# A mixture-of-experts macaron layer: windows of rows from anywhere in the first expert stage, outputs stored in place and gathered by token

## The chip, the cores and the metric

One core of a Trainium2 chip runs the whole program. The metric is the device time of one execution, in microseconds (us), as the median of several runs.

## The reference

The layer is a macaron: half a feed-forward, attention, half a feed-forward, each with its residual. `x` has 8 blocks of 512 tokens with 128 features in float32.

```python
x = x + 0.5 * ffn(layernorm(x))
x = x + attn(layernorm(x))
x = x + 0.5 * ffn(layernorm(x))
```

`attn` works in windows of 128 tokens: q, k, v, scores, the 32 largest scores of each row kept, softmax, values, a leaky ReLU, residual and layer norm. `ffn` is a mixture of eight experts with a shared one: a layer norm, a router of 8 logits, the two best experts of each token with softmax gates,

```python
for e in range(E):
    y = _swiglu(normed, gate_up_w[e], down_w[e])
    out = out + comb[:, e, None] * y
out = out + _swiglu(normed, shared_gate_up_w, shared_down_w)
```

where a routed expert has 384 hidden features. `comb` is zero for all but two experts of a token, so the kernel computes each expert on its own tokens only.

## The kernel before

**Stages.** The tokens are cut into two groups `g` of 4 blocks (2048 tokens). An expert stage is named `(key, g)`: `key` 0 is the feed-forward before attention, 1 the one after it. The stages run in the order (0,0), (0,1), (1,0), (1,1). Attention of group 0 lies beside stage (0,1), attention of group 1 beside stage (1,0). The shared expert (`shared`, L573) and the norms (`norm`, L532) are placed among them as filling.

**Routing** (`route`, L593). For the 2048 tokens of a group there are 4096 (token, expert) entries. They are sorted by expert into 4096 slots, that is `NS` = 32 tiles of 128 slots. VectorE (DVE) works out each expert's count (`cnt`), its first and last slot (`from_`, `last`), the slot of each entry (`pos`), and for each slot the token (`src`, L742). A tile can hold slots of several experts, so the work is a list of `NT` = 39 pairs (tile, expert), which covers every case. For each pair, DVE works out the expert's offsets (`row`, `off`), the tile's first column (`to`, which is `r.at`), and for each of its 128 rows the place where the output goes (`dst`, L826, from the chain `second`, `sx`, `held`, `sel`, `what`, `away`, L797 to L826).

**An expert stage** (`experts`, L832, and `pair`, L875). Per tile, GpSimd (POOL) issues an indirect DMA that gathers 128 normed token rows of 512 B from DRAM into `xg` (L846, four buffers of four tiles each). TensorE (PE) transposes them (`xTp`, L858), ScalarE (ACT) applies gamma and beta and writes them into `xT` (L863), which holds all 32 tiles of the stage. Per pair, PE multiplies the expert's gate and up weights `wt` with 128 columns of `xT` from column `r.at` (L924, three matmuls of 128x128 for `pg` and three for `pu`), ACT takes the silu (`s`, L932), DVE multiplies by up (L935), and PE multiplies by the down weights `ew` (`y`, L940). Stages (0,0) and (1,1) get `wt` by a DVE copy from a copy of all weights in SBUF (L899); the other two by a DMA on SyncE's queue, SP (L901). After four pairs ACT copies `y` to `yb` (L954), the last seven pairs one by one. Then POOL issues one indirect DMA per pair, the put (L962), which scatters the 128 rows of `yb` to the places in `dst`: row `1 + k*2048 + token` for a token's first or second expert. Rows of a pair that belong to another expert go to spare rows. After a put without other POOL work, a one-element memset stands before the next (L960).

**Back to the tokens.** `fetch_back` (L972) reads the two output rows of each token of a block with two plain DMAs of 256 KB, on SP for stage (0,0). They wait for all 39 puts. `combine` (L990, L999) adds them to `x` with the gates as factors, on DVE. `attention` and `norm(1, b)` follow for the block.

**What sets the order.** Every operation is handed to a planner (`Plan`, L96) with an engine, a cost, the operations that it needs and a due time. A list scheduler (`schedule`, L144) runs them on modelled engines, and the order that comes out is the order of each engine's queue on the chip. The queue of each engine is in order: a waiting instruction holds all behind it. The costs are in the calls (an indirect DMA on POOL: 1.28 for a gather, 1.33 for a put), the due times in the constants of L62 to L69: `PACE` spaces the gathers of the four stages, `LAG` the blocks of the attention, `SHARED`, `SHARED1`, `NORM_*`, `ROUTE_*`, `PAIRS`, `PUTS` and `FINISH` place the rest. Where the plan sees PE idle for long, it puts in matmuls whose result nobody reads (`unread`, L448).

```python
before_[2] = pool(1.28, fetch, [r.src, *rows], [(xg, j)], lat=3.6,
                  after=[(before_[2], pace)])
plan.op("POOL", 1.33, put, [(yb, i), r.dst], [(group, c * CH + i)], lat=3.4)
```

Of the kernel before, what the change touches and what calls it, by code (L numbers as in the profile page):

```python
# [8 lines left out]
F32 = mybir.dt.float32  # L9
F16 = mybir.dt.float16  # L10
U32 = mybir.dt.uint32
# [8 lines left out]
W = 4  # L20
# [24 lines left out]
COPIED = ((0, 0), (1, 1))  # L45
LAST = 4
LAST_ON_PE = (4, 6)

# [3 lines left out]
OVERLAP = {"PE": 0.0, "ACT": 0.08, "DVE": 0.07, "POOL": 0.0, "SP": 0.0}  # L52
TABLE_LOAD = 1.28
COLD, COLD_FACTOR = 26.0, 1.8

# [5 lines left out]

PACE = (1.79, 2.74, 2.27, 0.89)  # L62
LAG, STRETCH, ROUTE_STRETCH = 9.73, -0.34, 3.22
NORM_B, NORM_LAG, NORM_STRETCH = 7.11, 1.83, 1.14
SHARED = ((28.42, 6.74), (33.75, 24.46))
SHARED1 = ((114.02, 8.44), (5.88, 23.46))
ROUTE_B = 38.08
PAIRS, PUTS = 0.5, 4.89
FINISH = 18.87  # L69

# [182 lines left out]
def kernel(  # L253
# [35 lines left out]
                for t in (  # L289
                    "mx", "sm", "m0", "m1", "i0", "pr", "eq", "o0", "o1", "th", "own", "cnt",  # L290
                    "upto", "last", "from", "at", "posf", "pos", "lo", "hi", "lo2", "hi2", "hot",
                    "signed", "second", "held", "sx", "tl", "pairs", "end", "whose", "ex", "back",
                    "tile", "sel", "what", "away",
                )
# [11 lines left out]
    def dve(us, fn, r, w, **k):  # L306
        return plan.op("DVE", us, fn, r, w, **k)
# [95 lines left out]

    xT = const.tile([P, NS * P], F32, tag="xT", name="xT")
    zero = const.tile([1, H], F32, tag="zero", name="zero")
# [116 lines left out]
    def begin(key, g):  # L522


        r = routed[key, g] = Routing()
        r.rows = dram.tile([1 + GT, H], F32, tag=f"n{key}{g}", name=f"rows_{key}_{g}")
        r.ys = dram.tile([1 + 2 * GT + NTP * P, H], F32, tag=f"y{key}{g}", name=f"ys_{key}_{g}")
# [65 lines left out]
    def route(key, g):  # L593
# [124 lines left out]
        for q in range(0, 2 * GW, part):  # L718
# [29 lines left out]
        end, back = t("end", [P, 1, NE]), t("back", [P, NTP, 1])  # L748
        dve(0.17, lambda: ve.tensor_scalar(
            tl()[:, 0, :], last()[:, 0, :], float(P - 1), None, ALU.add), [last], [(tl, 0)])  # L750
        dve(0.17, lambda: ve.tensor_copy(tl()[:, 1, :], from_()[:, 0, :]), [from_], [(tl, 1)])
        dve(0.17, lambda: ve.tensor_scalar(tl(), tl(), 7, None, ALU.logical_shift_right),
            [(tl, 0), (tl, 1)], [(tl, 0), (tl, 1)])
        dve(0.17, lambda: ve.tensor_tensor(
            pairs()[:, 0, :], tl()[:, 0, :], tl()[:, 1, :], ALU.subtract),
            [(tl, 0), (tl, 1)], [pairs])
        dve(0.17, lambda: ve.scalar_tensor_tensor(
            pairs()[:, 0, :], cnt()[:, :, 0], 0.0, pairs()[:, 0, :], ALU.is_gt, ALU.mult),
            [cnt, pairs], [pairs])
        dve(0.22, lambda: ve.tensor_tensor(  # L760
# [4 lines left out]
            [end, pairs], [pairs])  # L765
        dve(0.17, lambda: ve.tensor_tensor(
            pairs()[:, 0, :], pairs()[:, 0, :], tl()[:, 1, :], ALU.subtract),
            [pairs, (tl, 1)], [pairs])
        dve(0.17, lambda: ve.tensor_tensor(
# [18 lines left out]
        dve(0.49, lambda: ve.tensor_reduce(back()[:, :, 0], whose(), AX.X, ALU.add),  # L788
            [whose], [back])
        dve(0.18, lambda: ve.tensor_tensor(  # L790
            tile_(), tno[:, :, 0], back()[:, :, 0], ALU.subtract), [back], [tile_])
# [16 lines left out]

        sel, what, away = t("sel", wide), t("what", [P, NTP]), t("away", [P, NTP])
        dst = r.dst = t("dst", [P, NTP], U32)  # L810
# [21 lines left out]
    def experts(key, g, pace):  # L832
# [7 lines left out]
        for c, n in enumerate(sizes):  # L840
            t0 = sum(sizes[:c])
            xg = buf([P, CH, H], "xg", f"xg_{nm}_{c}")
            for j in range(n):

                def fetch(t=t0 + j, j=j, xg=xg):
                    nc.gpsimd.indirect_dma_start(  # L846
                        xg()[:, j, :], None, r.rows,
                        bass.IndirectOffsetOnAxis(ap=r.src()[:, t : t + 1], axis=0),
                    )

                before_[2] = pool(1.28, fetch, [r.src, *rows], [(xg, j)], lat=3.6,
                                  after=[(before_[2], pace)])
                fetched.append(before_[2])
# [21 lines left out]
    def pair(r, key, g, t, pace, came, first, upto):  # L875
# [33 lines left out]

        lo, hi = max(0, first - NE + 1), min(upto, NS) - 1  # L910

        def up(p, c):
            if c == 0 and t == first:
# [5 lines left out]
                    )[1]  # L919
                    for to, a, b in ((r.off, 0, (NE - 1) * FF), (r.at, lo * P, hi * P))  # L920
                ]
# [29 lines left out]
        else:  # L951
# [3 lines left out]
            [(y, i) for i in range(a, b)], [(yb, i) for i in range(a, b)],  # L955
        )
        for i in range(a, b):
            def put(t=c * CH + i, i=i):
# [10 lines left out]

            plan.op("POOL", 1.33, put, [(yb, i), r.dst], [(group, c * CH + i)], lat=3.4)  # L970

    def fetch_back(key, b):  # L972
# [5 lines left out]
            buf([P, W, H], f"a{k + 1}" if key else "yg", f"yg_{key}_{b}_{k}") for k in range(2)  # L978
        ]
        ys_t = r.ys[1 : 1 + 2 * GT, :].rearrange("(k b p w) h -> b k p w h", k=2, p=P, w=W)  # L980
        written = [(f"ys_{key}_{g}", t) for t in range(NT)]
        for k in range(2):
# [7 lines left out]
    def combine(key, b, yg):  # L990
# [4 lines left out]
        for k in range(2):  # L995
# [7 lines left out]

            dve(1.5, run, [yg[k], (gates, k), xk], [xk])

# [228 lines left out]
```

## Time and profile before

| | |
|---|---|
| median of 6 runs | 641.13 us (638.38 to 648.55) |
| the profiled execution: its own time | 646.61 us |
| its span, first to last instruction | 644.8 us |
| granted TensorE clock, mean | 0.947 |
| busy | PE 532.0, weight loads 484.8, DVE 376.7, ACT 274.7, POOL 366.6 us |
| indirect DMAs on POOL | 128 gathers (L846), 156 puts (L962) |

By the times of their instructions the stages lie about here: routing and start until 42 us; (0,0) from 42 to 193 us, the last put at 193.45; (0,1) with attention of group 0 until 332; (1,0) with attention of group 1 until 494; (1,1) until 626; then the last outputs. The timeline lists an instruction with its start, its duration, its engine and line, its tiles, and in brackets the idle time of its engine before it with what ended that. A PE matmul's end is modelled, not measured.

### The profile page before, as it was taken

How to read it: one execution, taken by the hardware profiler on the slowest of the kernel's cores; microseconds unless marked ns; L12 is line 12 of the kernel's file. 1: busy time of each engine (PE TensorE's matmuls, PEld its weight loads, DVE VectorE, ACT ScalarE, POOL GpSimd, SP SyncE). 2: the span in 40 equal slices, each digit the busy share in tenths (PEclk: the TensorE clock that was granted, in tenths of full speed). 3: DMA queues.
4: the chain of work that ended last, by engine and by line, in shares of the span. 5: the costliest groups of instructions: out<-in, count | busy, mean ns of one | idle time of the engine just before them, and what ended most of it. 6: DMA issues, size and time to landing. Idle time of an engine off the chain costs nothing.

```text
span 644.8 us, 13493 instructions
## 1 busy us (share of the span) xinstructions
PE 532.0 (82%) x4064; PEld 484.8 (75%) x4064; DVE 376.7 (58%) x1440; ACT 274.7 (43%) x588; POOL 366.6 (57%) x484
## 2 busy tenths in 40 slices
PE   4996977686894999899998999898988486679986
PEld 3885867585783978789878788797877386669976
DVE  6594623564330788896498999773585254324412
ACT  5712312121231469787521688875542021222320
POOL 6136536454564578768636878686256446555450
PEclk9898978788998999999999999999899798899999
DMA  7911111101134844437536453456542312111016
GB/s 216 336 54 50 30 30 38 30 28 34 34 114 131 260 131 125 134 109 209 176 127 194 127 160 104 149 161 195 148 144 81 127 58 79 34 34 34 26 38 196
DMA packets 39611, 72.27 MB, mean 112 GB/s; under 512 B 7604, under 2 KB 17848, under 8 KB 39544
## 3 DMA queue, kind: packets, MB, share of 16 engines
q1 hardware_dynamic: 29880, 51.73, 26.2%
q0 software_dynamic: 9088, 18.63, 9.3%
q10 hardware_dynamic: 576, 1.05, 0.5%
q8 instruction: 38, 0.62, 0.4%
q14 instruction: 29, 0.24, 0.1%
HBM read 54.86 MB, written 16.52 MB: 111 GB/s over the span
## 4 chain that ended last, share of the span: by engine, by line
PE 58%; DVE 15%; another core or an unknown queue 8%; issue 6%; ACT 6%; DMA 3%; POOL 3%; DVEq 0%; SPq 0%; POOLq 0%; ACTq 0%
PE y L940 15%; PE pg L924 14%; PE pu L924 13%; DVE s L935 3%; PE ysh L588 2%; PE pus L582 2%; PE xTp L858 2%; PE pgs L579 2%; PE lg L563 2%; DVE wt L899 2%; POOL ys L962 2%; DVE tk L1088 1%; DMA yg<-ys 1%; DVE x L999 1%
## 5 line engine op out<-in xcount | busy, mean ns | idle before, releaser
L962 POOL DMA_INDIRECT ys<-yb,dst x156 | 158.8, 1018 | 170.2 <-ACT yb L954 144.3
L940 PE MATMUL y<-ew,s 128*128 x936 | 142.8, 293 | 65.9 <-DVE s L935 54.2
L940 PEld LDWEIGHTS y<-ew,s 128*128 128x128 f32 x936 | 126.0, 204 | 78.2 <-DVE s L935 46.4
L846 POOL DMA_INDIRECT xg<-rows,src x128 | 127.1, 993 | 68.0 <-issue 34.8
L932 ACT ACTIVATE s<-pg 128x384 f32<-128x384 f32 x156 | 75.2, 490 | 191.2 <-PE pg L924 73.4
L924 PE MATMUL pg<-xT,wt 128*128 (+1 forms) x936 | 138.5, 286 | 14.9 <-ACT xT L863 7.8
L924 PEld LDWEIGHTS pg<-xT,wt 128*128 128x128 f32 x936 | 122.9, 199 | 23.5 <-issue 11.0
L924 PE MATMUL pu<-xT,wt 128*128 (+1 forms) x936 | 134.1, 281 | 0.9 <-DVE s L935 0.9
L899 DVE COPY wt<-egu 128x768 f32 x78 | 44.4, 570 | 139.8 <-PE pu L924 57.6
L924 PEld LDWEIGHTS pu<-xT,wt 128*128 128x128 f32 x936 | 121.1, 197 | 2.1 <-DVE s L935 1.1
L935 DVE TENSOR_TENSOR s<-pu,s 128x384 f32<-128x384 f32 x156 | 85.0, 550 | 58.3 <-PE pu L924 20.8
L954 ACT COPY yb<-y 128x512 f32<-128x512 f32 (+1 forms) x60 | 26.1, 436 | 54.2 <-PE y L940 31.8
L999 DVE SCALAR_TENSOR_TENSOR x<-yg,gates,x 128x128 f32<-128x128 f32 x112 | 35.5, 380 | 12.2 <-DMA yg<-ys 12.2
L863 ACT ACTIVATE xT<-xTp,gb 128x512 f32<-128x512 f32 (+2 forms) x34 | 25.4, 753 | 32.0 <-PE xTp L858 25.2
L448 PEld LDWEIGHTS unread<-ident 128*128 128x128 f32 x264 | 31.0, 192 | 1.9 <-issue 1.9
L448 PE MATMUL unread<-ident 128*128 128x128 f32 x264 | 31.8, 275 | 0.0
L1088 DVE MATCH_REPLACE8 tk<-am,tk 128x128 f32<-128x128 f32 x96 | 25.3, 273 | 0.0
L499 ACT ACTIVATE n<-x,nb,rstd 128x128 f32<-128x128 f32 x56 | 22.8, 485 | 4.5 <-DVE nb L479 4.5
L563 PEld LDWEIGHTS lg<-rwT,nT 128*128 128x128 f32 x128 | 19.7, 236 | 6.4 <-ACT nT L554 5.8
L858 PE MATMUL xTp<-ident,xg 128*128 128x128 f32 x128 | 22.2, 298 | 2.5 <-DMA xg<-rows,src 1.4
L563 PE MATMUL lg<-rwT,nT 128*128 128x8 f32 x128 | 19.7, 284 | 4.3 <-ACT nT L554 4.3
L581 ACT ACTIVATE ss<-pgs 128x512 f32<-128x512 f32 x16 | 9.5, 596 | 28.0 <-PE pgs L579 20.1
(177 smaller groups left out, 698.1 us busy)
## 6 DMA issues: line engine op xcount, KB each, us to landing
wt<-in_expert_gu SPq DMA_DIRECT2D x78, 384.0 KB
yg<-ys SPq DMA_DIRECT2D x28, 256.0 KB
rows<-n SPq DMA_DIRECT2D x16, 256.0 KB
egu<-in_expert_gu SPq DMA_DIRECT2D x8, 384.0 KB
ys<-yb,dst POOLq DMA_INDIRECT x156
x<-in_x SPq DMA_DIRECT2D x8, 256.0 KB
xg<-rows,src POOLq DMA_INDIRECT x128
out_x<-x SPq DMA_DIRECT2D x8, 256.0 KB
```

The costliest lines, as they stand in the source:

```text
L448: plan.idle = lambda: nc.tensor.matmul(unread, ident, ident, start=True, stop=True)
L563: nc.tensor.matmul(lg()[:, w, 0:NE], nT()[:, w, :], rwT, start=True, stop=True)
L846: nc.gpsimd.indirect_dma_start(xg()[:, j, :], None, r.rows, bass.IndirectOffsetOnAxis(ap=r.src()[:, t : t + 1], axis=0),)
L858: nc.tensor.transpose(tp()[:, w, :], xg()[:, w, :], ident)
L899: nc.vector.tensor_copy(to, egu[:, bass.ds(row, 2 * FF)])
L924: nc.tensor.matmul(p()[:, f, :], wt()[:, c * NF + f, :], xT[:, bass.ds(offs[1], P)], start=True, stop=True,)
L932: act(0.49, lambda: nc.scalar.activation(s(), pg()[:, 0:NF, :], AF.Silu), [pg], [s], table="silu")
L935: dve(0.56, lambda: nc.vector.tensor_tensor(s(), pu()[:, 0:NF, :], s(), ALU.mult), [pu, s], [s])
L940: nc.tensor.matmul(y()[:, j, :], s()[:, f, :], ew[:, bass.ds(offs[0] + f * H, H)], start=(f == 0), stop=(f == NF - 1),)
L962: ins = nc.gpsimd.indirect_dma_start(r.ys, bass.IndirectOffsetOnAxis(ap=r.dst()[:, t : t + 1], axis=0), yb()[:, i, :], None,).ins
L999: nc.vector.scalar_tensor_tensor(xs[b][:, w, :], yg[k]()[:, w, :], gates()[:, k, q : q + 1], xs[b][:, w, :], ALU.mult, ALU.add,)
L1088: ve.match_replace(tk()[:, w, :], m8()[:, w, :], src()[:, w, :], TAKEN)
```

## The change

In stage (0,0) alone (`WINDOWS`):

- A pair is no longer a tile with one of its experts. It is a window of 128 consecutive slots that begins anywhere: expert e gets `ceil(cnt/128)` windows, which begin at its first slot. There are still `NT` = 39 windows. `to` is then a column of `xT` that need not be a multiple of 128, and `xT` gets 128 more columns, zeroed.
- All 128 output rows of a window are stored where the window stands in the list: `ys` has 39 * 128 rows, and a plain DMA on SP writes a chunk of four windows at once (the last seven alone). The 39 puts of this stage go.
- `route` leaves out the chain of `dst` in this stage. Instead it adds to the slot of each entry what its expert's windows are shifted by, and keeps the two rows of each token in `want`.
- `fetch_back` gathers by `want`: for each block 2 x 4 indirect DMAs on POOL of 128 rows, 32 in all, in place of 8 plain DMAs. `combine` waits for the four gathers of its half.

The planner's cost of every indirect DMA, in all stages, becomes 1.72 (`INDIRECT`) for 1.28 and 1.33, and the due times are others. So the order of the instructions changes in all stages. `sel` shares its buffer with `whose`.

```diff
+WINDOWS = ((0, 0),)
+INDIRECT = 1.72
-PACE = (1.79, 2.74, 2.27, 0.89)
-LAG, STRETCH, ROUTE_STRETCH = 9.73, -0.34, 3.22
-NORM_B, NORM_LAG, NORM_STRETCH = 7.11, 1.83, 1.14
-SHARED = ((28.42, 6.74), (33.75, 24.46))
-SHARED1 = ((114.02, 8.44), (5.88, 23.46))
-ROUTE_B = 38.08
-PAIRS, PUTS = 0.5, 4.89
-FINISH = 18.87
+PACE = (1.79, 3.63, 1.5, 1.75)
+LAG, STRETCH, ROUTE_STRETCH = 10.08, -1.11, 7.26
+NORM_B, NORM_LAG, NORM_STRETCH = 11.74, 1.11, 2.32
+SHARED = ((28.42, 5.57), (35.54, 33.74))
+SHARED1 = ((73.75, 8.44), (5.88, 23.46))
+ROUTE_B = 34.16
+PAIRS, PUTS = -0.52, 2.74
+FINISH = 6.94
...
-    xT = const.tile([P, NS * P], F32, tag="xT", name="xT")
+    xT = const.tile([P, (NS + 1) * P], F32, tag="xT", name="xT")
+    nc.gpsimd.memset(xT[:, NS * P :], 0.0)
...
+        if r.windows:
+            dve(0.18, lambda: ve.scalar_tensor_tensor(
+                tile_(), tno[:, :, 0], float(P), back()[:, :, 0], ALU.mult, ALU.subtract),
+                [back], [tile_])
+            dve(0.18, lambda: ve.tensor_scalar(
+                to(), tile_(), float(NS * P), None, ALU.min), [tile_], [to])
+            plan.floor = max(floor, found.due + PUTS)
+            dve(B, lambda: ve.tensor_tensor(
+                at(), at(), pairs().to_broadcast(full), ALU.add), [at, pairs], [at])
+            for k, o in ((0, o0), (1, o1)):
+                dve(B, lambda o=o: ve.tensor_tensor(eq(), o(), at(), ALU.mult), [o, at], [eq])
+                dve(B, lambda k=k: ve.tensor_reduce(posf()[:, k, :], eq(), AX.X, ALU.add),
+                    [eq], [(posf, k)])
+            want = r.want = t("want", [P, 2 * GW, 1], U32)
+            before_[3] = dve(0.18, lambda: ve.tensor_copy(
+                want()[:, :, 0], posf().rearrange("p k w -> p (k w)")),
+                [(posf, 0), (posf, 1)], [want])
+            return
...
-                before_[2] = pool(1.28, fetch, [r.src, *rows], [(xg, j)], lat=3.6,
+                before_[2] = pool(INDIRECT, fetch, [r.src, *rows], [(xg, j)], lat=3.6,
...
+        if r.windows:
+            to = r.ys[(c * CH + a) * P : (c * CH + b) * P, :].rearrange("(i p) h -> p i h", p=P)
+            load(0.6, lambda: to, lambda: yb()[:, a:b, :], [(yb, i) for i in range(a, b)],
+                 [(group, c * CH + i) for i in range(a, b)], lat=3.0)
+            return
...
-            plan.op("POOL", 1.33, put, [(yb, i), r.dst], [(group, c * CH + i)], lat=3.4)
+            plan.op("POOL", INDIRECT, put, [(yb, i), r.dst], [(group, c * CH + i)], lat=3.4)
...
+        if r.windows:
+            for k in range(2):
+                for w in range(W):
+                    def fetch(k=k, w=w, q=k * GW + i * W + w):
+                        nc.gpsimd.indirect_dma_start(
+                            yg[k]()[:, w, :], None, r.ys,
+                            bass.IndirectOffsetOnAxis(ap=r.want()[:, q, :], axis=0),
+                        )
+                    pool(INDIRECT, fetch, [r.want, *written], [(yg[k], w)], lat=3.6)
+            return yg
...
-            dve(1.5, run, [yg[k], (gates, k), xk], [xk])
+            came = [(yg[k], w) for w in range(W)] if routed[key, g].windows else [yg[k]]
+            dve(1.5, run, [*came, (gates, k), xk], [xk])
```

More of the change, by code (lines that the diff above doesn't have):

```diff
@@ L292 @@
                     "signed", "second", "held", "sx", "tl", "pairs", "end", "whose", "ex", "back",
-                    "tile", "sel", "what", "away",
+                    "tile", "what", "away", "want",
                 )
@@ L526, in begin @@
         r.rows = dram.tile([1 + GT, H], F32, tag=f"n{key}{g}", name=f"rows_{key}_{g}")
-        r.ys = dram.tile([1 + 2 * GT + NTP * P, H], F32, tag=f"y{key}{g}", name=f"ys_{key}_{g}")
+        r.windows = (key, g) in WINDOWS
+        n = NT * P if r.windows else 1 + 2 * GT + NTP * P
+        r.ys = dram.tile([n, H], F32, tag=f"y{key}{g}", name=f"ys_{key}_{g}")
         load(0.3, lambda: r.rows[0:1, :], lambda: zero, (), [("rows", key, g, -1)], lat=3.0)
@@ L748, in route @@
         end, back = t("end", [P, 1, NE]), t("back", [P, NTP, 1])
[L749 to L759, printed above, removed]
+        if r.windows:
+            dve(0.17, lambda: ve.tensor_scalar(
+                tl()[:, 0, :], cnt()[:, :, 0], float(P - 1), None, ALU.add), [cnt], [(tl, 0)])
+            dve(0.17, lambda: ve.tensor_scalar(
+                tl()[:, 0, :], tl()[:, 0, :], 7, None, ALU.logical_shift_right),
+                [(tl, 0)], [(tl, 0)])
+            dve(0.17, lambda: ve.tensor_copy(pairs()[:, 0, :], tl()[:, 0, :]), [(tl, 0)], [pairs])
+        else:
+            dve(0.17, lambda: ve.tensor_scalar(
+                tl()[:, 0, :], last()[:, 0, :], float(P - 1), None, ALU.add), [last], [(tl, 0)])
+            dve(0.17, lambda: ve.tensor_copy(tl()[:, 1, :], from_()[:, 0, :]), [from_], [(tl, 1)])
+            dve(0.17, lambda: ve.tensor_scalar(tl(), tl(), 7, None, ALU.logical_shift_right),
+                [(tl, 0), (tl, 1)], [(tl, 0), (tl, 1)])
+            dve(0.17, lambda: ve.tensor_tensor(
+                pairs()[:, 0, :], tl()[:, 0, :], tl()[:, 1, :], ALU.subtract),
+                [(tl, 0), (tl, 1)], [pairs])
+            dve(0.17, lambda: ve.scalar_tensor_tensor(
+                pairs()[:, 0, :], cnt()[:, :, 0], 0.0, pairs()[:, 0, :], ALU.is_gt, ALU.mult),
+                [cnt, pairs], [pairs])
         dve(0.22, lambda: ve.tensor_tensor(
@@ L765, in route @@
             [end, pairs], [pairs])
-        dve(0.17, lambda: ve.tensor_tensor(
-            pairs()[:, 0, :], pairs()[:, 0, :], tl()[:, 1, :], ALU.subtract),
-            [pairs, (tl, 1)], [pairs])
+        if r.windows:
+            dve(0.17, lambda: ve.scalar_tensor_tensor(
+                pairs()[:, 0, :], pairs()[:, 0, :], float(P), from_()[:, 0, :],
+                ALU.mult, ALU.subtract), [pairs, from_], [pairs])
+        else:
+            dve(0.17, lambda: ve.tensor_tensor(
+                pairs()[:, 0, :], pairs()[:, 0, :], tl()[:, 1, :], ALU.subtract),
+                [pairs, (tl, 1)], [pairs])
         dve(0.17, lambda: ve.tensor_tensor(
@@ L789, in route @@
             [whose], [back])
+        if r.windows:
[15 more added lines that the diff above has]
+                [(posf, 0), (posf, 1)], [want])
+            plan.floor = floor
+            return
         dve(0.18, lambda: ve.tensor_tensor(
@@ L807, in route @@
             [signed, second], ["held"])
-        sel, what, away = t("sel", wide), t("what", [P, NTP]), t("away", [P, NTP])
+        sel, what, away = whose, t("what", [P, NTP]), t("away", [P, NTP])
         dst = r.dst = t("dst", [P, NTP], U32)
@@ L910, in pair @@
         lo, hi = max(0, first - NE + 1), min(upto, NS) - 1
+        end = P * min(NS, upto - 1) if r.windows else P * hi
         def up(p, c):
@@ L919, in up @@
                     )[1]
-                    for to, a, b in ((r.off, 0, (NE - 1) * FF), (r.at, lo * P, hi * P))
+                    for to, a, b in ((r.off, 0, (NE - 1) * FF), (r.at, lo * P, end))
                 ]
@@ L956, in pair @@
         )
+        if r.windows:
+            to = r.ys[(c * CH + a) * P : (c * CH + b) * P, :].rearrange("(i p) h -> p i h", p=P)
+            load(0.6, lambda: to, lambda: yb()[:, a:b, :], [(yb, i) for i in range(a, b)],
+                 [(group, c * CH + i) for i in range(a, b)], lat=3.0)
+            return
         for i in range(a, b):
@@ L979, in fetch_back @@
         ]
+        written = [(f"ys_{key}_{g}", t) for t in range(NT)]
+        if r.windows:
+            for k in range(2):
[7 more added lines that the diff above has]
+            return yg
         ys_t = r.ys[1 : 1 + 2 * GT, :].rearrange("(k b p w) h -> b k p w h", k=2, p=P, w=W)
-        written = [(f"ys_{key}_{g}", t) for t in range(NT)]
         for k in range(2):
```

## The prediction, made before the change was run

> **What bounds the kernel now.** I read the page first: engine shares, then the groups of the two indirect DMAs.
>
> ```profile
> PE 532.0 (82%) x4064; PEld 484.8 (75%) x4064; DVE 376.7 (58%) x1440; ACT 274.7 (43%) x588; POOL 366.6 (57%) x484
> PEclk9898978788998999999999999999899798899999
> L962 POOL DMA_INDIRECT ys<-yb,dst x156 | 158.8, 1018 | 170.2 <-ACT yb L954 144.3
> L846 POOL DMA_INDIRECT xg<-rows,src x128 | 127.1, 993 | 68.0 <-issue 34.8
> ```
>
> PE is the busiest, with a full clock in the middle and a lower one in the first and last expert stage. A put or a gather takes about 1.0 us and 0.3 us of issue, and puts mostly wait for ACT: POOL looks like no bound. Then the busy times by stage, for the stretches 42 to 193 us, stage (0,0), and 193 to 332 us, stage (0,1) with attention:
>
> ```profile
> 42.00:193.00 151.00, 117.80 (x865) 106.24 (x864) 68.82 (x179) 39.30 (x75) 82.84 (x107) 0.91 0.14 43
> 193.00:332.00 139.00, 123.84 (x962) 111.81 (x961) 98.81 (x439) 87.31 (x191) 92.81 (x113) 0.98 0.51 156
> ```
>
> In (0,0) no engine is full (PE 118 of 151 us, clock 0.91, although DVE has 69 and POOL 83). So I looked at what happens around one chunk, in the timeline of POOL, ACT and DVE:
>
> ```profile
> 148.25 1.08 POOL L962 DMA_INDIRECT ys<-yb,dst  x1 [0.22 <-issue]
> 149.63 1.01 POOL L846 DMA_INDIRECT xg<-rows,src  x1 [0.30 <-issue]
> 150.95 0.96 POOL L846 DMA_INDIRECT xg<-rows,src  x1 [0.31 <-issue]
> 152.21 0.94 POOL L846 DMA_INDIRECT xg<-rows,src  x1 [0.30 <-issue]
> 152.94 0.49 ACT L932 ACTIVATE s<-pg 128x384 f32<-128x384 f32 x1 [5.99 <-PE pu L924]
> 153.46 0.94 POOL L846 DMA_INDIRECT xg<-rows,src  x1 [0.30 <-issue]
> 155.83 0.56 DVE L899 COPY wt<-egu 128x768 f32 x1 [5.01 <-remote]
> 155.96 0.49 ACT L932 ACTIVATE s<-pg 128x384 f32<-128x384 f32 x1 [2.53 <-remote]
> ```
>
> While POOL issues eight indirect DMAs without a pause (144.4 to 154.4 us), ACT idles 6.0 and 2.5 us and DVE 5.0 us, although the matmuls that they wait for stand as done. The trace's record of semaphore updates says why: PE's semaphore doesn't rise from 148.6 to 152.9 and from 152.9 to 155.8 us, and then several times within 0.2 us. Set beside POOL's unbroken runs, such silences follow their length: runs of 7, 9, 7, 8 and 7 in this stage have 7.3, 5.8, 7.3, 7.2 and 7.3 us of silence, runs of 4 in (1,1) 0 to 3.0 us, in multiples of some 2.9 us. Why it is so the trace doesn't show; I use it as a relation. PE can go on for a while, then starves. From 42 to 206 us its pauses between matmul starts of over 1.5 us sum to 35.5 us. Seven stretches at clock 0.5 follow them, 34.1 us in all, worth half, 17.1. Together 52.6 us.
>
> The end of the stage, in SP's timeline and the chain:
>
> ```profile
> 184.53 21.08 SPq L901 DMA_DIRECT2D wt<-in_expert_gu  x5
> 205.72 0.84 SPq L317 DMA_DIRECT2D yg<-ys  x2
> ```
>
> ```profile
> 197.35 7.91 another core or an unknown queue
> ```
>
> The last put is issued at 193.45, but the read-back stands behind weight loads in SP's queue until 205.72, and the first combine runs at 212.27.
>
> **The change part by part.**
>
> (a) *39 puts go from POOL in (0,0).* From 42 to 206 us POOL issues 87 indirect DMAs: 39 puts and 48 gathers, 16 of them for (0,1). Puts and gathers join into runs of 7 to 9; without puts a chunk has a run of about 4. By share, 39/87 of 52.6 is 23.6 us. Lower end, nothing: puts were hidden and the silences stay with the gathers. Upper end, by runs of 4 in (1,1) (PE pauses of 1.65, 1.56 and 1.61 us, clock 1.0): about 45.8 us over 8 chunks is 5.7 each, 1.6 would remain, 33 gained. I take 24, the share in the stage itself.
>
> (b) *Handover.* Before, the last `yb` copy ends at 191.95 and the first combine starts at 212.27: 20.3 us. After: one store on SP (0.4 issue, landing as in the read issued at 213.43 and landed at 215.9, 2.5), eight gathers at 1.26 (to the start of the last, 8.8) and 2.4 to landing (gather at 115.12, complete by 117.5): 14.1. That is 6 gained, of which some 4 lie in the pauses already counted: 2. If a last store stands behind a weight load in SP's queue, as the read-back did, up to 9 are lost instead. SP has no other transfer from 31 to 184 us, so the first 8 stores delay nothing there.
>
> (c) *32 gathers on POOL in (0,1).* They wait for all stores, and behind them in POOL's queue stand the (0,1) gathers, its puts, and the `rstd` and add operations of attention; PE's transposes wait for those. POOL in 193 to 332: 92.8 busy plus 62 DMAs by 0.3 is 111 us of 139. Add 32 by 1.26, 40, and take off 8 gathers that can move before 193 (10): 141. POOL becomes full, where PE (124) and DVE (99) were not. Price: 2 if it packs perfectly; 15 if the order is rigid, since the last block's outputs come 3 by 10 us after the first where the reads were issued over 15 us. I take 8, between the two, as no row is nearer to either.
>
> (d) *Runs of eight in (0,1).* Four runs. Nearest by length, the run of eight at 536.9 to 547.1 us: a pause of 4.7 and a half-clock stretch of 3.4, 6.4 us; four are 26. Nearest by place, runs of four at 249.4 and 261.2 us in (0,1): no pause over 1.5 us, as attention work lies beside. The place is nearer: 4 by 1.5, 6 us. Bounds 0 and 26.
>
> (e) *Edits that I cost at nothing.* DVE in `route`: out go eleven operations of `dst` (0.24, 0.19, 0.41, 0.41, 0.18, 0.48, 0.49, 0.47, 0.19, 0.19, 0.21: 3.5 us) and two of the pair count (0.3), in come six for `want` (0.29, two of 0.30, two of 0.29, 0.20: 1.7): 2.1 us less, covered because the first gather at 42.27 waits for `src`, which comes earlier; without cover a 2 us gain. The memset of `xT` (about 0.2 us) lies in POOL's wait of 23.7 us for `src`. Matmuls are as many, with the same shapes.
>
> (f) *The other order.* The 1.72 and new due times move instructions in all stages. No row prices this. Gain at most as in the largest pause, 9.7 us after the run of 14 at 491 to 508.7 us, if (1,1)'s wider pace breaks it; loss at most as the unread matmuls of (1,0) again, 12.7 us. I take 0.
>
> [...]
>
> Sum: -24 - 2 + 8 + 6 = -12 us. Against the profiled execution's own 646.6 us (span 644.8 and 1.8 around it) that is 634.6. It ran 5.5 above the median, so against 641.1 it is 629.
>
> **The rivals.**
>
> R1, slower: POOL becomes the bound of (0,1). For it: 141 us of work in a 139 us stretch, in one in-order queue, 32 gathers at its front. Against it: 16 gathers of (0,1) can be ahead already, and PE has those pairs to work on. With (c) at 15 and (d) at 26 the sum is -24 - 2 + 15 + 26 = +15: 656. It decides once (c) and (d) together pass 26 us.
>
> R2, no difference: the puts were hidden. For it: POOL waits for ACT 49 us in 42 to 193 before puts, and the silences run on into the gathers. With (a) at 8, (b) 2 and (c) alone at 8: -2, 639. Against it: runs of puts only have silences too (2.9 at 590.3, 3.0 at 600.4).
>
> R3, a larger gain: short runs cost as in (1,1), (a) at 33, and packing is good, (b) 2, (c) 2, (d) 0: -33, 608.
>
> **How the numbers follow.** Forecast 0.39, with its own range 619 to 639; R1 0.30; R2 0.16; R3 0.15. Predicted 629. The range takes in R3 and R1 with a little of (f): 606 to 660. A measurement of this kernel can tell about 1%, 6.4 us: faster below 634.7, slower above 647.5. Faster: R3 and most of the forecast, 0.15 + 0.36 = 0.51. Slower: R1 and the forecast's tail of bad order, 0.31. The rest, 0.18, is within 1%.
>
> **What would show it.** (a) Right if (0,0) from the first gather to the last `yb` copy shrinks from 150 us by about 20, with POOL runs of four and fewer ACT and DVE waits put down to "remote"; wrong if the chunks keep their 16 us pace. (b) First combine some 14 us after the last copy; wrong if SP's stores stand behind weight loads. (c) and (d) POOL's busy share in (0,1) near full, and the route of (1,0), whose first gather is now at 340.9, at most 14 us later against the start of attention; wrong if PE waits for transposes of late gathers there. (f) Wrong if stages (1,0) and (1,1), 162 and 132 us now, change by more than 10 us. The forecast falls if the puts were not what broke PE's pace, or if 32 gathers cost more in (0,1) than 39 puts did in (0,0).

## The result, and the profile after

| | before | after |
|---|---|---|
| median | 643.77 us (46 runs) | 723.39 us (20 runs) |
| ratio | | 1.129, interval 1.126 to 1.132 |
| profiled execution, its own time | 646.6 us | 717.85 us |
| its span | 644.8 us | 716.1 us |

The forecast was 629 us with a range of 606 to 660. The kernel became 12.9% slower. The 641.13 us above are the first six of the 46 runs of the kernel before.

From the page of the changed kernel: busy times, granted clock by slice, and the groups of the gathers, the puts, the unread matmuls and the new gathers; the last line is the unread matmuls of the kernel before.

```profile
PE 611.3 (85%) x4770; PEld 569.4 (80%) x4770; DVE 374.9 (52%) x1433; ACT 278.7 (39%) x588; POOL 358.2 (50%) x458
PEclk9996999699898999999999999997989879889999
L888 POOL DMA_INDIRECT xg<-rows,src x128 | 130.6, 1020 | 126.2 <-PE xTp L900 37.7
L1010 POOL DMA_INDIRECT ys<-yb,dst x117 | 117.7, 1006 | 125.3 <-ACT yb L997 106.2
L454 PE MATMUL unread<-ident 128*128 128x128 f32 x970 | 121.0, 281 | 5.3 <-issue 5.3
L1033 POOL DMA_INDIRECT yg<-ys,want x32 | 31.7, 989 | 9.3 <-issue 8.9
```

```profile
L448 PE MATMUL unread<-ident 128*128 128x128 f32 x264 | 31.8, 275 | 0.0
```

The new operations cost what the prediction took: 32 gathers of 0.99 us, 39 puts fewer. POOL is no busier than before (358.2 us against 366.6). PE is, by 79 us, and its unread matmuls alone are 89 us more: 970 with 121.0 us, where the kernel before has 264 with 31.8 us. The planner puts these where its own model sees PE idle, so their number says that the plan itself is longer, before any chip has run it: 606.9 us against 516.7 (the table of the eight combinations below).

The stages, by the last copy into `yb`, show where the time went. In each row: the stretch, its length, the busy time of PE, PEld, DVE, ACT and POOL, the clock, the DMA share and GB/s. The second view counts the unread matmuls alone. The third has the last three stretches of the kernel before; the prediction shows its first two.

```profile
42.00:174.00 132.00, 108.33 (x839) 100.64 (x838) 63.48 (x167) 37.55 (x73) 52.27 (x53) 0.90 0.20 54
174.00:365.00 191.00, 173.38 (x1378) 160.98 (x1378) 110.58 (x471) 91.45 (x193) 112.24 (x135) 0.96 0.36 110
365.00:543.00 178.00, 154.88 (x1208) 142.59 (x1207) 112.17 (x499) 94.19 (x209) 101.14 (x125) 0.94 0.43 131
543.00:688.00 145.00, 119.79 (x947) 115.08 (x946) 53.24 (x123) 31.69 (x63) 77.50 (x107) 0.92 0.18 55
688.00:716.00 28.00, 22.91 (x206) 22.72 (x204) 4.38 (x16) 1.17 (x2) 0.11 (x1) 0.96 0.35 115
```

```profile
42.00:174.00 132.00, 0.83 (x6) 0.75 (x6) 0.90 0.20 54
174.00:365.00 191.00, 43.82 (x368) 42.88 (x368) 0.96 0.36 110
365.00:543.00 178.00, 27.38 (x202) 24.99 (x202) 0.94 0.43 131
543.00:688.00 145.00, 25.88 (x193) 24.81 (x194) 0.92 0.18 55
688.00:716.00 28.00, 17.55 (x158) 17.36 (x156) 0.96 0.35 115
```

```profile
332.00:492.00 160.00, 143.18 (x1156) 129.58 (x1155) 127.14 (x543) 94.43 (x211) 105.26 (x124) 0.99 0.48 147
492.00:625.00 133.00, 100.62 (x769) 95.85 (x769) 48.36 (x110) 31.48 (x63) 70.57 (x102) 0.91 0.19 58
625.00:645.00 20.00, 14.43 (x130) 14.23 (x128) 4.38 (x16) 1.44 (x3) 1.43 (x3) 0.99 0.51 165
```

| stretch | before | after | difference |
|---|---|---|---|
| (0,0) | 151 | 132 | -19 |
| (0,1) | 139 | 191 | +52 |
| (1,0) | 160 | 178 | +18 |
| (1,1) | 133 | 145 | +12 |
| last outputs | 20 | 28 | +8 |
| sum | 603 | 674 | +71 |

The sum is +71 us where the medians differ by 80: the execution profiled before was 3 us over its median, the one after 6 us under it. Stage (0,0) did become shorter. Everything after it became longer, also (1,0) and (1,1), in which the change touches no operation, only the planner's costs and due times. In (0,1) POOL is busy 112 of 191 us: it did not become the bound.

What happens in (0,1) is read from the timeline, first PE, then POOL (start, duration, operation, count).

```profile
249.76 1.06 PE L1131 MATMUL psc<-kT,qT 128*128 128x128 f32 x8
250.65 13.34 PE L454 MATMUL unread<-ident 128*128 128x128 f32 x118
...
266.10 4.18 PE L454 MATMUL unread<-ident 128*128 128x128 f32 x36
...
277.82 9.32 PE L454 MATMUL unread<-ident 128*128 128x128 f32 x82
```

```profile
175.02 0.94 POOL L888 DMA_INDIRECT xg<-rows,src  x1 [0.30 <-issue]
...
301.16 0.99 POOL L888 DMA_INDIRECT xg<-rows,src  x1 [0.17 <-issue]
302.46 0.95 POOL L888 DMA_INDIRECT xg<-rows,src  x1 [0.31 <-issue]
...
313.59 0.96 POOL L888 DMA_INDIRECT xg<-rows,src  x1 [0.50 <-issue]
317.97 1.02 POOL L888 DMA_INDIRECT xg<-rows,src  x1 [0.16 <-issue]
319.29 0.95 POOL L888 DMA_INDIRECT xg<-rows,src  x1 [0.30 <-issue]
```

These are row gathers of (0,1): the 23rd at 175.02 us, then some of the last nine, from 301 us on. Between the two POOL issues no row gather; the largest such pause in (0,1) before was 19 us. Without their rows there are few pairs to multiply, and from 250 us on PE is given fillers (the unread matmuls), 118 in one piece. None of these nine gathers had long to wait itself (0.16 to 0.50 us): the list had put them behind 32 gathers of the combine, spread from 177 to 274 us, and behind puts. So this is the order of a queue, not a queue that is full. The pause comes with the 32 gathers: in (0,1) it is 86 to 126 us in every trace that has them, whatever the cost and the due times, and 13 to 32 us in every trace without them.

The changed list takes three things together: windows, a cost of 1.72 for an indirect DMA, and new due times. The experiments take them apart. Letters in the expectations: O is the theory that the new order (cost and due times) makes the loss; W that the windows themselves do, through their 32 gathers on POOL; F that the unread matmuls do.

### The profile page after: what moved, and what is told of

Same layout as the page of the kernel before. It is cut to its first block, busy times and chain, and to the rows that moved or that the text cites. A ratio compares the mean times of both kernels' runs of the same rounds, so it can differ in the third digit from the quotient of the medians.

```text
span 716.1 us, 14902 instructions
## 1 busy us (share of the span) xinstructions
PE 611.3 (85%) x4770; PEld 569.4 (80%) x4770; DVE 374.9 (52%) x1433; ACT 278.7 (39%) x588; POOL 358.2 (50%) x458
## 4 chain that ended last, share of the span: by engine, by line
PE 67%; another core or an unknown queue 11%; DVE 10%; ACT 5%; issue 5%; DMA 1%; SPq 0%; POOL 0%; DVEq 0%; ACTq 0%
PE pg L967 14%; PE y L983 14%; PE pu L967 13%; PE unread L454 12%; DVE tk L1148 2%; PE xTp L900 2%; PE ysh L596 2%; PE pgs L587 2%; DVE s L978 2%; DVE am L1144 1%; PE pus L590 1%; PE lg L571 1%; ACT n L505 1%; DMA x<-in_x 1%
## 5 line engine op out<-in xcount | busy, mean ns | idle before, releaser
L888 POOL DMA_INDIRECT xg<-rows,src x128 | 130.6, 1020 | 126.2 <-PE xTp L900 37.7
L1010 POOL DMA_INDIRECT ys<-yb,dst x117 | 117.7, 1006 | 125.3 <-ACT yb L997 106.2
L967 PEld LDWEIGHTS pg<-xT,wt 128*128 128x128 f32 x936 | 124.5, 202 | 27.1 <-ACT xT L905 12.7
L967 PE MATMUL pu<-xT,wt 128*128 (+1 forms) x936 | 137.1, 284 | 2.3 <-issue 1.8
L967 PEld LDWEIGHTS pu<-xT,wt 128*128 128x128 f32 x936 | 123.6, 201 | 3.0 <-issue 3.0
L454 PE MATMUL unread<-ident 128*128 128x128 f32 x970 | 121.0, 281 | 5.3 <-issue 5.3
L454 PEld LDWEIGHTS unread<-ident 128*128 128x128 f32 x970 | 116.2, 197 | 9.6 <-issue 9.6
L1058 DVE SCALAR_TENSOR_TENSOR x<-yg,gates,x 128x128 f32<-128x128 f32 x112 | 31.3, 347 | 14.6 <-DMA yg<-ys 14.6
L1033 POOL DMA_INDIRECT yg<-ys,want x32 | 31.7, 989 | 9.3 <-issue 8.9
```

Source lines behind the costliest of these rows:

```text
L454: plan.idle = lambda: nc.tensor.matmul(unread, ident, ident, start=True, stop=True)
L888: nc.gpsimd.indirect_dma_start(xg()[:, j, :], None, r.rows, bass.IndirectOffsetOnAxis(ap=r.src()[:, t : t + 1], axis=0),)
L967: nc.tensor.matmul(p()[:, f, :], wt()[:, c * NF + f, :], xT[:, bass.ds(offs[1], P)], start=True, stop=True,)
L1010: ins = nc.gpsimd.indirect_dma_start(r.ys, bass.IndirectOffsetOnAxis(ap=r.dst()[:, t : t + 1], axis=0), yb()[:, i, :], None,).ins
L1033: nc.gpsimd.indirect_dma_start(yg[k]()[:, w, :], None, r.ys, bass.IndirectOffsetOnAxis(ap=r.want()[:, q, :], axis=0),)
```

## Experiments: cost, due times and windows apart

The runs were made in five groups, each on another chip, and the same program does not run equally long in all of them: the kernel before took 530.47 and 529.22 us in the first and the last group (chips 12 and 2), 659.6, 642.99 and 640.52 in the three between (chips 9, 5 and 14). No chip was used twice, so the runs do not tell the chip from the time at which it ran. Every ratio is against the kernel before in the same group, and the text says where two kernels of different groups are set beside each other.

The edits, each on the changed kernel:

```diff
# windows off
-WINDOWS = ((0, 0),)
+WINDOWS = ()
# the old cost
-INDIRECT = 1.72
+INDIRECT = 1.28
-            plan.op("POOL", INDIRECT, put, ...
+            plan.op("POOL", 1.33, put, ...
# the old due times: lines PACE to FINISH as before
```

**windows_only** (old cost, old due times):

> Windows, stores in place and gathers in stage (0,0), with the costs (1.28 and 1.33) and the due times of before. Theory O (the loss is the order: longer planned DMAs and other due times): the structure alone does about what was forecast, 625 to 645 us. Theory W (the loss is the windows: 32 gathers fill POOL in (0,1)): 690 to 725 us. Unread matmuls in the program: 494 instructions against 264 before and 970 after.

Measured: 558.94 us, ratio 1.051 (1.043 to 1.059). The expectations of this group are times beside 641 us, and here the kernel before took 530.47; as ratios, O expects 0.98 to 1.01 and W 1.08 to 1.13, and the run lies between.

**order_only** (windows off; cost 1.72, new due times):

> Puts and read-back of before in all stages, but the planner's cost of 1.72 and the due times of after. 1002 instructions of unread matmuls. Theory O: 700 to 725 us, nearly the whole loss. Theory W: 640 to 655 us.

Measured: 619.11 us, ratio 1.166 (1.160 to 1.173). O expects 1.09 to 1.13: the loss is larger than O's.

**cost_only** (windows off, old due times; cost 1.72):

> As before, with only the planner's cost of an indirect DMA at 1.72; due times of before; 1002 instructions of unread matmuls. Theory O with the cost as its main part: 690 to 720 us. If the due times are the main part instead: 640 to 660. Theory W: 640 to 650.

Measured: 624.60 us, ratio 1.176 (1.169 to 1.183), above the 1.08 to 1.12 expected of the cost as the main part.

**before_again** (all three taken back; what is left of the change is 128 more columns of `xT` with their memset, and a shared buffer):

> Before once more, for its trace on the chip of this call: with no windows, the costs and due times of before (only the buffer of sel shared and xT 128 columns longer). 530 us if the chip is as in the last call, 640 us if it is as in the first. If the silences of PE's semaphore come from the program (POOL's unbroken runs), the trace shows as many as the first one, 260 us in 71; if they come from the chip, far fewer at 530 us, about 85 us as with the windows alone.

Measured: 662.24 us, ratio 1.005 (1.002 to 1.009). What the factors leave over is worth about half a per cent. The trace has 70 silences of PE's semaphore, 276 us, where the first one has 71 with 260 us; as the kernel before took 660 us here too, this does not tell program from chip.

**after_again** (the changed kernel unchanged):

> After on the same chip as the other variants. Theory O: its order costs most. By the sum of the parts (windows alone 1.05, cost and due times alone 1.17) 1.20 to 1.23 of before, 640 us against 530; if the windows take back part of what the order costs, 1.10 to 1.15, 585 to 610.

Measured: 732.26 us, ratio 1.111 (1.105 to 1.118): the windows take back part of what the order costs.

**due_only** (windows off, old cost; new due times):

> As before, with the due times of after alone: costs 1.28 and 1.33, no windows, 508 instructions of unread matmuls. If the due times matter next to the cost: 545 to 565 us against 530. If they were chosen for another cost and hurt as much as the cost itself: 600 and more. If they do nothing: 530.

Measured: 700.47 us, ratio 1.066 (1.057 to 1.075).

**windows_due** (the changed kernel with the old cost alone):

> Windows with the due times of after, but costs of 1.28 and 1.33: 580 instructions of unread matmuls. Against after this takes away the planner's 1.72 alone. If the 1.72 is the main loss: 555 to 575 us against 530. If not: 595 to 610, as after.

Measured: 695.17 us, ratio 1.057 (1.051 to 1.064): as expected if the 1.72 is the main loss.

**windows_cost** (windows and cost 1.72, old due times):

> The windows and the cost 1.72, with the old due times: the last combination of the three parts. If the cost is the main cause, this is far above windows alone: 1.15 to 1.20 (the plan's own length is 634 us, against 607 for the changed kernel and 517 before), and the due times of the changed kernel win some of it back (to 1.11 to 1.13). If windows, cost and due times each only add their share, 1.05 x 1.17 = 1.23.

Measured: 754.46 us, ratio 1.172 (1.162 to 1.182), as expected of the cost as the main cause.

All eight combinations, with the length that the kernel's own plan has for each (this is what the planner reckons, no measurement):

| windows | cost | due times | plan, us | unread matmuls | ratio |
|---|---|---|---|---|---|
| no | 1.28 | old | 516.7 | 264 | 1.005 |
| no | 1.28 | new | 546.8 | 508 | 1.066 |
| no | 1.72 | old | 630.1 | 1002 | 1.176 |
| no | 1.72 | new | 621.4 | 1002 | 1.166, 1.172 |
| yes | 1.28 | old | 546.3 | 494 | 1.051, 1.057 |
| yes | 1.28 | new | 561.3 | 580 | 1.057 |
| yes | 1.72 | old | 634.1 | 1094 | 1.172 |
| yes | 1.72 | new | 606.9 | 970 | 1.111, 1.129 |

Three things follow. First, the cost is the largest single part: by itself 17.6%, on top of the windows 11.5 points (1.057 to 1.172). In the changed kernel, whose due times win some of that back, taking the cost alone back gives 732.26 to 695.17 us in one group, 37 us. Second, the windows alone lose 5 to 6%, with the order priced as before. Third, the parts do not add up, and what the windows bring depends on the list: with the cost of 1.72 and the old due times they change nothing that can be told (1.176 without, 1.172 with), and with 1.72 and the new due times they are a gain (1.166 and 1.172 without, 1.111 and 1.129 with); these ratios are of different groups. In one group, due_only and windows_due differ in nothing but the windows: 700.47 and 695.17 us, 1.066 and 1.057, with intervals that overlap. Only on the list of before do the windows lose. The plan's length tells much of this ahead: in the first group the time lies within 3% of it (516.7 and 530.47, 546.3 and 558.94, 621.4 and 619.11, 630.1 and 624.60 us).

1.72 is dearer than what the chip shows. In the changed kernel's timeline gathers follow one another at 1.25 us:

```profile
177.15 0.94 POOL L1033 DMA_INDIRECT yg<-ys,want  x1 [1.19 <-issue]
178.40 0.95 POOL L1033 DMA_INDIRECT yg<-ys,want  x1 [0.30 <-issue]
179.65 0.94 POOL L1033 DMA_INDIRECT yg<-ys,want  x1 [0.31 <-issue]
```

In most of an expert stage a chunk of four pairs has four gathers and four puts: 8 times 1.72 is 13.8 us in the plan, and 8 times 1.28 some 10.2. A planner that takes POOL for the bound puts other work, and fillers, into the pauses that it sees; the chip then runs them in that order. That this is how the cost acts is read from the plan and from the count of fillers (264 to 1002 by the cost alone), not shown instruction by instruction.

## Experiments: fillers, or what they fill

The edit is one line:

```diff
-    plan.idle = lambda: nc.tensor.matmul(unread, ident, ident, start=True, stop=True)
+    plan.idle = lambda: None
```

**after_no_unread**:

> After with no unread matmul put in at all (970 instructions fewer, which write a bank that nobody reads). If those matmuls stand in PE's queue ahead of work that could run (theory F, filler): 650 to 680 us. If they only fill pauses in which PE would wait anyway: 715 to 735 us, with a lower granted clock.

Measured: 593.04 us where the kernel before took 530.47, ratio 1.118 (1.109 to 1.126). As a ratio F expects 1.01 to 1.06, and fillers that only fill 1.12 to 1.15 at a lower clock: the run is at the edge of the second, at a clock of 0.917 where the other traces of its group have 0.989 to 0.995.

**order_no_unread**:

> The list of order_only (no windows; cost 1.72 and the new due times), with the unread matmuls left out, which compute nothing that is used. If the fillers only fill pauses that the order makes, the time stays at that of order_only, 1.15 to 1.18, and PE shows pauses in their place, at a lower granted clock. If issuing 1002 fillers is what costs (some 120 us of busy PE), it falls to 1.05 or less.

Measured: 700.03 us where the kernel before took 642.99, ratio 1.086 (1.077 to 1.096), far below the 1.166 of order_only in another group. So both were run again in one group, with a control.

**order_again** and **order_no_unread_again**:

> The new order alone (cost 1.72, due times of the changed kernel, no windows), again, beside its twin without fillers on one chip. If the order's loss does not depend on the chip: 1.15 to 1.18, as in order_only. If on a chip with many silences of PE's semaphore the fillers run where PE would have waited anyway, less: 1.10 to 1.13.

> order_again without its 1002 unread matmuls (nothing that is used is left out). order_no_unread gave 1.0864. If the fillers themselves cost time, because the list places them by its own clock and the chip runs ahead of it, the difference to order_again is 0.05 or more on one chip; if they only fill pauses, it is within 0.02.

Measured: 751.86 us, ratio 1.172 (1.164 to 1.180), and 698.03 us, ratio 1.090 (1.080 to 1.099). **before_no_unread**:

> The kernel before without its 264 unread matmuls (33 us of busy PE). Control for the fillers: if those of the kernel before cover pauses, 0.99 to 1.02, at a lower granted clock; if fillers cost their own time, 0.95 to 0.97.

Measured: 643.98 us, ratio 1.004 (0.999 to 1.008).

The pages of order_again and order_no_unread_again, busy times and the engines' shares of the chain that ended last:

```profile
PE 634.2 (84%) x4802; PEld 584.1 (78%) x4802; DVE 377.3 (50%) x1440; ACT 274.1 (36%) x586; POOL 367.6 (49%) x495
PE 69%; DVE 9%; another core or an unknown queue 9%; ACT 6%; issue 6%; DMA 1%; DVEq 0%; SPq 0%; ACTq 0%
```

```profile
PE 528.2 (76%) x3800; PEld 475.6 (68%) x3800; DVE 377.7 (54%) x1440; ACT 274.1 (39%) x586; POOL 371.0 (53%) x495
PE 49%; DVE 14%; another core or an unknown queue 9%; ACT 9%; issue 8%; POOL 6%; DMA 3%; SPq 1%; DVEq 0%; POOLq 0%; ACTq 0%
```

In this group half of the order's loss is the fillers (0.082 of 0.172), and PE's share of the chain falls from 69 to 49% when they go; in order_again fillers are 13% of the chain. The likely reading is that they fill pauses that the plan has and the chip does not have, so that a real matmul stands behind fillers in PE's queue. The granted clock falls too when they go, from 0.928 to 0.896, so 8% is what is left of their cost after that. The other half, 9%, is the order itself. Those of the kernel before, 264, cost nothing that can be seen, so "fillers only fill" was right for that list and wrong for this one.

**after_no_unread_again**:

> The changed kernel without its 970 unread matmuls, again: after_no_unread gave 1.1176 on a chip on which the kernel before took 530 us. If fillers cost the changed kernel what they cost the order alone (1.172 against 1.090 on one chip), it falls to 1.04 to 1.07 where the kernel before takes some 640 us; if the earlier value holds on every chip, 1.11 to 1.13.

Measured: 593.80 us where the kernel before took 529.22, ratio 1.122 (1.117 to 1.128), as in after_no_unread. Both of these fell into groups in which the kernel before takes some 530 us, and their clock is 0.915 to 0.917. The changed kernel with its fillers was not run there, nor this one where the kernel before takes 640 us, so what the fillers cost the changed kernel itself stays open. Without them the loss remains.

## Experiments: what the windows cost by themselves

**windows_again** (the program of windows_only):

> Windows alone (spans of rows, stores in place, 32 gathers), with the list priced and dated as before: the cost of an indirect DMA 1.28 and 1.33, the old due times. A repeat of windows_only beside other kernels. If the loss of the windows is the order of POOL in (0,1), where the 32 gathers of the combine push the last rows' gathers of (0,1) back, it is there on any chip: 1.04 to 1.06, and the pause in (0,1)'s gathers is 80 us or more again. If the relation of the prediction's step (a) held (PE's semaphore silences follow POOL's unbroken runs), a chip with many silences would give some 24 us back in (0,0): 1.01 or less.

Measured: 678.97 us, ratio 1.057 (1.048 to 1.066), with a pause of 110 us in (0,1)'s gathers: what was expected of the order of POOL in (0,1), not of the prediction's (a).

**windows_planned** (the same with due times searched for this list, by the length of the kernel's own plan):

> Windows with the cost of before (1.28), and with due times searched for this list by its own plan: the plan's length is 531.3 us where the due times of before give 546.3 with windows and 516.7 without. If the loss of the windows is only that due times made for another list put POOL's work in the wrong order, the time comes down by the plan's 15 us: 1.02 to 1.03 of before. If the 32 gathers cost POOL time that no order hides, it stays at 1.05. The price of the windows with the best order found is then what is left over 1.00; under 1.00 would mean that the puts taken from POOL in (0,0) pay after all.

```diff
-PACE = (1.79, 2.74, 2.27, 0.89)
-LAG, STRETCH, ROUTE_STRETCH = 9.73, -0.34, 3.22
+PACE = (0.3, 2.73, 2.03, 0.79)
+LAG, STRETCH, ROUTE_STRETCH = 7.91, -14.77, 3.12
...
```

Measured: 669.55 us, ratio 1.040 (1.031 to 1.049). That is 9 us less, of the plan's 15, and more than the 1.02 to 1.03 expected if due times were all. The best order that was found for the windows still loses.

**windows_plain_back** (windows_again with plain reads in place of the 32 gathers; it leaves out the gathering by token, so it adds rows that are not those of its tokens):

> Windows with the cost and due times of before, but the combine of (0,0) reads the stored rows with four plain loads in each half as before, in place of the 32 indirect gathers: the rows that it adds are not those of its tokens. It has the gain of step (a), 39 puts less on POOL in (0,0), without the price of steps (c) and (d). If (a) is right, 0.96 to 0.98 (24 us). If the 32 gathers are what windows cost, at least 1.04 less than windows alone, so 1.01 or under, and the combine of (0,0) takes about 19 us again where windows take 80. If the loss of windows is in the stores in place or the unaligned spans, it stays at 1.04 to 1.06.

```diff
-        if r.windows:
+        if False:
             for k in range(2):
                 for w in range(W):
                     def fetch(...
...
-            came = [(yg[k], w) for w in range(W)] if routed[key, g].windows else [yg[k]]
+            came = [yg[k]]
```

Measured: 661.34 us, ratio 1.033 (1.026 to 1.041), under the 1.04 to 1.06 and over the 1.01 that were expected. The combine of (0,0), in windows_again and then in windows_plain_back: count, shortest, median and longest in ns, first and last start.

```profile
L1058 DVE SCALAR_TENSOR_TENSOR x<-yg,gates,x x32: 335/346/549, 209.1 to 289.5; 128x128 f32<-128x128 f32 x32
```

```profile
L1058 DVE SCALAR_TENSOR_TENSOR x<-yg,gates,x x32: 320/344/1726, 191.9 to 212.1; 128x128 f32<-128x128 f32 x32
```

With gathers the combine takes 80 us, with plain reads 20, as before (19). The stages by the last `yb` copy are, before, windows_again and windows_plain_back: (0,0) 150, 144, 138; (0,1) 140, 176, 146; (1,0) 160, 165, 168; (1,1) 133, 125, 143 us. So the 32 gathers cost (0,1) 30 us and the whole 0.024, some 15 us; the ratios are of two groups. And without them 39 puts less on POOL, with nothing in return, are still a loss of 3.3%: (0,0) wins 12 us and (0,1), (1,0) and (1,1) lose 24; beside before_no_unread, which ran in the same group, it is 19 and 27.

**plain_back_planned** (the same, with due times searched for it; the plan's length falls from 530.6 to 513.8 us):

> windows_plain_back (stores in place, no indirect gathers in the combine, so the rows added are not those of the tokens) with due times searched for this list: the plan's length falls from 530.6 us to 513.8, where the kernel before has 516.7. If the 3.3% that windows_plain_back still loses is the order alone, it falls to 0.99 to 1.00, and if the 39 puts taken from POOL in (0,0) are worth the 24 us of step (a), to 0.96 to 0.97. If unaligned spans or stores cost time of their own, it stays at 1.02 or more.

Measured: 528.01 us where the kernel before took 529.22, ratio 0.998 (0.995 to 1.001).

Its stages, (0,0), (0,1), (1,0), (1,1), in the columns of above:

```profile
42.00:146.00 104.00, 100.49 (x894) 95.72 (x893) 68.53 (x181) 38.26 (x74) 52.69 (x52) 1.00 0.24 70
146.00:270.00 124.00, 121.61 (x967) 110.99 (x966) 98.66 (x458) 88.70 (x193) 81.60 (x99) 1.00 0.53 168
270.00:416.00 146.00, 140.06 (x1145) 128.58 (x1144) 123.08 (x523) 94.11 (x210) 102.81 (x124) 0.98 0.52 160
416.00:509.00 93.00, 90.18 (x790) 88.51 (x789) 49.67 (x113) 31.86 (x62) 73.78 (x104) 1.00 0.27 85
```

In this group PE is busy 100 of 104 us in (0,0) and 96 to 98% of the time in the other stages: PE is the bound by its busy time, whose ends are modelled, and puts taken from POOL are worth nothing. Stores in place and spans that begin anywhere thus run at the speed of the kernel before in this group. So the 3.3% of windows_plain_back is no cost of these two, as far as a ratio carries over from its group to this one. In this group there were no long silences of PE's semaphore to shorten (6 us in (0,0)). Left open: whether this list would win something where the kernel before takes 640 us.

No version was found that beats the kernel before.

## Why the prediction was wrong

**The step that failed is (f), "The other order".** It said "No row prices this", bounded it by -9.7 and +12.7 us and took 0. The order alone, cost and due times without the windows, measured +111 us (order_again: 751.86 against 640.52). In the changed kernel the cost alone is worth 37 us (after_again less windows_due), and on the list of before the due times alone 6.6%. The bound came from one pause and one count of fillers in the trace of before; but the order is remade in every stage, and its price is no row of a trace. Two things in the diff could have warned: 1.72 against the 1.25 to 1.28 us that the rows of before show for an indirect DMA, and a cost that applies to 277 operations of the changed kernel in four stages, where the windows touch one. The test that the prediction named for (f), that (1,0) and (1,1) change by more than 10 us, came out against it: +18 and +12.

The windows' own sum, (a) to (d), -12 us, failed on one list and not on another. With the new due times and the old cost the windows alone gave -5 us, not clear of noise (windows_due less due_only, one group); on the list of before they gave +36 us (678.97 against 642.99). The prediction added (a) to (d) and (f) as if each had a price of its own; they do not.

Point by point:

- *(a) 39 puts, -24.* The stage shrank by 19 us, near the 24, but in part by luck. PE has 7 us less of shared expert work in the stage (20.3 us before, 13.2 after), which stands elsewhere in the new order. The time at half clock, a third of the 52.6 us of which (a) took its share, did not change (27.3 us in both). The signs that it named came out mixed: ACT and DVE wait 41 us for "remote", where they waited 42, and POOL's runs are four in four chunks, with runs of 15, 12 and 8 beside them. The pair that differs in the windows alone, due_only and windows_due, has 15 us less in (0,0) and 20 us more in (0,1). So the stage does gain, and the time came back later; without the gathers, and with an order made for that list, nothing is left in a group without long silences (0.998). The relation behind it, silences of PE's semaphore after runs of POOL's indirect DMAs, is not general: see the last section. A stage that gets shorter is no gain until the end of the kernel shows it.
- *(b) Handover, 14.1 for 20.3.* It became 22.3 us. The eight gathers start at 177.15 to 185.90 as worked out, but PE stands meanwhile: no matmul starts from 183.3 to 189.7 us. The chain of the changed kernel:

```profile
177.41 0.57 DVE s L978
177.97 0.70 issue
178.67 0.02 ACT s L975
178.70 9.82 another core or an unknown queue
```

  and DVE, in its order, has products of (0,1) before the first combine:

```profile
189.06 0.56 DVE L978 TENSOR_TENSOR s<-pu,s 128x384 f32<-128x384 f32 x1 [2.65 <-ACT s L975]
192.71 0.56 DVE L978 TENSOR_TENSOR s<-pu,s 128x384 f32<-128x384 f32 x1 [3.09 <-PE pu L967]
195.26 0.56 DVE L978 TENSOR_TENSOR s<-pu,s 128x384 f32<-128x384 f32 x1 [1.99 <-PE pu L967]
195.73 1.13 DVE L1058 SCALAR_TENSOR_TENSOR x<-yg,gates,x 128x128 f32<-128x128 f32 x4
```

  By the prediction's own 2.4 us from a gather's start to landing, the rows of all eight were there at about 188.3; the combine came 7.4 us later. It needs only the first four, started by 180.90, so eight in the sum was too many. The stores did not stand behind SP's weight loads, the last went out at 173 us: the named risk did not come.
- *(c) and (d), +8 and +6.* As a sum near, by luck: the 32 gathers cost about 15 us (windows_again less windows_plain_back). The picture was wrong. POOL is not full, it is busy 112 of 191 us; the combine is drawn out from 20 to 80 us and the last row gathers of (0,1) come behind it. The stall of 9.82 us beside the first run of eleven indirect DMAs (three gathers of rows and eight of the combine, 172.5 to 186.9 us) is dearer than the 1.5 us that (d) took from the quiet runs of four, and more than the 6.4 us of its dear end; only this one was followed.
- *(e) route, memset, buffers at nothing.* Not contradicted: before_again, which has the memset and the buffers, is at 1.005. DVE has 1.8 us less of busy time, where 2.1 were worked out.
- *The price of one gather*, 1.26 us in (b) and (c), held: 989 ns each (L1033), at the 1.25 us of the timeline above; the gathers of rows took 993 ns before.
- *R1, slower.* Right in sign and wrong in mechanism: POOL did not become the bound, and (c) with (d), some 15 us, did not pass 26. *R2* says that the puts were hidden; plain_back_planned shows that for one group of runs, without the gathers. *R3* is refuted.

What is shown: cost, due times and windows each lose on the list of before, the cost most; that the windows do not lose with the new due times and the old cost; that the gathers bring the long pause of (0,1). What rests on ratios of two groups: what the windows bring under 1.72, the gathers' share of the windows' loss, and that an order made for plain_back takes its loss away. What is only argued: which pairs of instructions stand the wrong way round under 1.72. And the loss of windows_planned, 4.0%, is not fully split: the gathers give about 2.4 points of it, the rest is order or is left open.

## What to carry to other kernels

Where a planner makes the order, a cost in it is a change of the whole kernel: check it against the measured pitch, and count the idle fillers of the new plan, before the operations that were meant to change are summed up. A shorter stage is not a gain until the next ones are seen to keep it; here the next stages' work was placed for the old handover. To judge a change and its retuning, run them apart.

## What was not expected of the hardware

The kernel before took 530 us in two groups of runs and 640 to 660 in the other three and in the first result, the same program. It has no trace at 530 us, but other programs ran in both kinds of group, and in their traces the difference goes with silences of PE's semaphore: stretches of over 2.4 us without an update. From the trace's record of semaphore updates, in stage (0,0) from 42 us to the last `yb` copy, with the pauses of over 1.5 us between PE's matmul starts:

| kernel | (0,0), us | silences, us | PE pauses, us | longest runs of indirect DMAs | kernel before in its group |
|---|---|---|---|---|---|
| before | 150 | 61 | 27 | 15, 14, 9 | 643.77 |
| after | 131 | 43 | 20 | 15, 12, 8 | 643.77 |
| windows_again | 144 | 49 | 26 | 16, 16, 8 | 642.99 |
| windows_plain_back | 138 | 42 | 23 | 16, 12, 8 | 640.52 |
| windows_only | 108 | 3 | 0 | 32, 16, 4 | 530.47 |
| order_only | 123 | 8 | 0 | 16, 11, 8 | 530.47 |
| plain_back_planned | 104 | 6 | 0 | 32, 16, 4 | 529.22 |

The 8 us of order_only are stretches in which PE ran fillers. Where there are silences, there are fewer of them with fewer puts, which goes with the shorter (0,0) of (a). But windows_only and windows_again are one program, and at the same pitch of indirect DMAs (1.28 us in both) runs of up to 32 leave 3 us of silence in one group, and runs of up to 16 leave 49 in the other. So POOL's runs are not enough to make a silence; something that differs between the groups is needed too. The groups are different chips, and no run here shows what in the chip, or in the time of the run, it is. The granted clock goes with it, windows_only and then windows_again:

```profile
core 0: 558.2 us, clock 0.995
```

```profile
core 0: 671.5 us, clock 0.932
```

The ratios barely feel it: windows 1.051 and 1.057, the order 1.166 and 1.172.
